# One visit of the multiplier for the last 64 middle units of two neighbouring expert blocks

## The chip, the cores and the metric

The kernel runs on one core of a Trainium2 chip. The core has a matrix engine (TensorE, "PE" in the profile; its weight loads are listed apart as "PEld"), a vector engine (VectorE, "DVE"), a scalar engine (ScalarE, "ACT"), a general engine (GpSimd, "POOL") and an engine that here only issues transfers (SyncE, "SP"). Each engine works through its own list in order; where one needs another's result it waits on a semaphore. Matrix results land in PSUM, eight banks that hold 128 x 512 float32 numbers each; everything else is in SBUF. The metric is device time in microseconds (us) of one execution.

## The reference: attention, then a mixture of nine experts

Shapes: `x` is 4 x 1024 x 256, that is 4096 tokens of width 256.

```python
x = x + xattn(ctx, layernorm(x), scale, shift)   # 16 heads, 77 keys a batch
h = layernorm(x)                                  # 4096 x 256
probs = softmax(h @ Wr)                           # 9 experts
w, idx = top_k(probs, 2); w = w / sum(w)
hidden = silu(h @ Wg[e]) * (h @ Wu[e])            # 704 middle units of expert e
out = x + sum over the token's two e of w_e * (hidden @ Wd[e])
```

All of it is float32. The 704 middle units are 5 x 128 + 64, and that odd 64 is what the change is about.

## The kernel before

The first part, up to some 340 us of the trace, is attention and routing: it finishes the new `x`, decides each token's two experts, and writes lists of tokens by expert into HBM. The second part works through 40 *blocks*. A block is a set of tokens with its experts; `blocks` (L1240 to L1257) holds the order as triples (token tiles, number, kind):

- *pair* blocks have 256 tokens of one expert, two token tiles `h` = 0, 1 of 128. There are 26: six early ones (blocks 0 to 5), whose places are known before all tokens are routed, and later ones of the kinds quad/quad2 (two neighbours that share one load of weights) and pair;
- *thin* blocks ("one") have 128 tokens of one expert;
- flex and quart blocks have 128 tokens of two or four experts, worked by column tiles of the multiplier.

The order of the kinds after the early blocks is the string at L1243, in which Q stands for quad, quad2; P for a pair, O for a thin block, F for flex, X for quart. Five more blocks (Q O Q O P) follow it.

Step `j` of the main loop does this. `fetch` (L1574) issues the loads: weights of block j+2, rows of tokens of block j+3, lists further ahead; SP issues weights in order, through `load` (L1338), into three buffers for Wg and Wu and four for Wd. `hidden_pair` (L1414) multiplies the block's turned tokens `xT` by Wg and Wu in six chunks `f`. A chunk is 128 middle units and fills a bank `pg`: ACT takes silu of one half (L1427), DVE multiplies it by the other half into `hid` (L1428). The sixth chunk has 64 units: 64 columns of Wg stand beside 64 of Wu, so one product gives gate on rows 0 to 63 and up on rows 64 to 127, and L1432 and L1433 make rows 64 to 127 of `hid[:, NF, :]` from it. Rows 0 to 63 of that slice are zeros, set once, and so are those of Wd's buffers.

Between chunks, DVE has other work in the same queue: in the early blocks `pump` (L1551) lets up to 12 instructions of the routing of the last token group and of the late blocks' tables go by after each chunk; from step 6 on, `turning` (L1389) gives it three 32 x 32-square transposes after each chunk, 16 a block, which turn the next block's tokens. In steps 1 to 5, `turn` (L1401) turns the next block's tokens on the multiplier instead, with four instructions into a PSUM bank `px`, after the block's `hidden_pair`.

Then, still in step j, `down(j - 1)` (L1508) multiplies the *previous* block's hidden units by Wd: for each token tile six accumulating products of 128 rows, `f` = 0 to 5, the last with the 64 rows of zeros. ACT scales the result by the token's weight (`co`, L1519) and POOL adds the rows into the output (`adding`, L1537). So PE always has twelve products of the block before to do while ACT and DVE finish the present block's last chunk. The schedule is written out by hand: the engines' queues are in the order of the calls.

PSUM: five banks in a ring (`mm_tile`, L133) for all `pg`, `px` and the routing's products, and three named banks: `sc0` for `px`, `sc1` and `sc2` for `down`.

Of the kernel before, what the change touches and what calls it, by code (L numbers as in the profile page):

```python
# [21 lines left out]
def kernel(  # L22
# [99 lines left out]

    ps_mm = ctx.enter_context(tc.tile_pool(name="ps_mm", bufs=5, space=bass.MemoryType.PSUM))
    ps_sc = ctx.enter_context(tc.tile_pool(name="ps_sc", bufs=1, space=bass.MemoryType.PSUM))
# [6 lines left out]
    BH = B // 2  # L131

    def mm_tile(name):  # L133
        return ps_mm.tile([P, TB], F32, tag="mm", name=name)

# [1106 lines left out]
    uppers, turn_set = {}, 0  # L1242
    order = "QO PF PO QX PO QF PF PO QX PO QF PF"  # L1243
    for step in order.replace(" ", ""):
# [11 lines left out]
    uppers[LAST] = [turn_set % SETS]  # L1256


    begun = {}
# [6 lines left out]
    wgus, downs, xTs, cos = {}, {}, {}, {}  # L1266
    hids, wds, yins, ids = [], [], [], []
    late = {}
# [14 lines left out]
    def open_experts():  # L1283
        for name, bufs in (("wpool", LEAD + 1), ("fpool", 1), ("spool", 2)):
            pools[name] = ctx.enter_context(tc.tile_pool(name=name, bufs=bufs))
        f = pools["fpool"]
        hids.extend(f.tile([P, NF + 1, TS], F32, name=f"hid{i}") for i in range(2))
        wds.extend(f.tile([P, NF + 1, D], F32, name=f"wd{i}") for i in range(NB_W))
        yins.extend(f.tile([P, 2, D], F32, name=f"yin{i}") for i in range(NB_Y))

        ids.extend(f.tile([P, b[0], WORDS], I32, name=f"ids{j}") for j, b in enumerate(blocks))
        for t in hids + wds:
            nc.gpsimd.memset(t[0:64, NF, :], 0.0)
        for t in yins:
            nc.gpsimd.memset(t, 0.0)
# [6 lines left out]
    def weights(j, in_parts=False):  # L1302
# [16 lines left out]
        at = PARTS[kind] * i  # L1319
        parts = load(tabs[kind][0][0:1, at : at + 1], w, d)  # L1320
        if in_parts:
# [15 lines left out]

    def load(number, w, d):  # L1338
        e = nc.values_load(number, engines=[mybir.EngineType.SP], min_val=0, max_val=E - 1)
# [13 lines left out]
        )  # L1353
        nc.sync.dma_start(
            out=d[64:128, NF, :], in_=wd[bass.ds(e, 1), NF * P : FF, :].rearrange("o p d -> (o p) d")
        )
        yield True
# [43 lines left out]
    def turn(j):  # L1401

        nh, xT = blocks[j][0], turned_tile(j)
        px = ps_sc.tile([P, TB], F32, tag="sc0", name=f"px{j}").rearrange("p (c t) -> p c t", c=C)
        for c in range(C):
# [8 lines left out]
    def hidden_pair(j, also={}, upcoming=iter(())):  # L1414

        (w,), xT, hid = wgus.pop(j), xTs.pop(j), hids[j % 2]
        for f in range(NF + 1):
# [13 lines left out]
            else:  # L1431
                nc.scalar.activation(sl[64:128, :], pg[0:64, 0, :], AF.Silu)  # L1432
                nc.vector.tensor_tensor(  # L1433
                    hid[64:128, NF, :], pg[64:128, 0, :], sl[64:128, :], ALU.mult
                )
            pump()
# [71 lines left out]
    def down(j):  # L1508
        ds, hid, nh = downs.pop(j), of(hids, j), blocks[j][0]
        co = cos[j] = pools["spool"].tile([P, 2, D], F32, tag="co", name=f"co{j}", bufs=3)  # L1510
        for h in range(nh):
            po = down_tile(j, h)
            for f in range(NF + 1):
                for d, rows in zip(ds, lanes(ds)):
                    at = slice(h * P + rows.start, h * P + rows.stop)
                    nc.tensor.matmul(  # L1516
                        po[rows, :D], hid[:, f, at], d[:, f, :], start=(f == 0), stop=(f == NF)
                    )
            nc.scalar.activation(  # L1519
                co[:, h, :], po[:, :D], AF.Copy, scale=ids[j].bitcast(F32)[:, h, 1:2]  # L1520
            )

    def down_tile(j, h):
# [213 lines left out]


    delayed = []
    for j in range(LAST):  # L1740
# [60 lines left out]
```

## Time and profile before

| | |
|---|---|
| time, median of 3 | 853.81 us (852.67 to 854.43) |
| the profiled execution | 852.54 us, span 850.8 us, granted TensorE clock 0.998 |
| PE busy | 840.8 us, 99% of the span |
| weight loads (beside PE) | 674.9 us, 79% |
| DVE busy | 596.7 us, 70% |
| ACT busy | 380.7 us, 45% |
| POOL busy | 313.1 us, 37% |
| DMA | 208 GB/s on average |

A group line gives line, engine, operation, names of output and input, the array's rows x columns, the operand's partitions x elements and the count, then total busy time and mean ns. A timeline line gives start, length, engine, line, operation, names, shapes, count, and in brackets the engine's idle time before it and what ended that. A float32 product of the program is two MATMUL records in the trace. Records of PE overlap, since its work is pipelined and its ends are modelled: the pace is read from one start to the next.

### The profile page before, as it was taken

The page shows a single profiled execution, that of the slowest core. Times are in us where ns is not written, and L with a number is a line of the kernel's source. Part 1 is how long each engine was busy: PE and PEld are TensorE (multiplying, and loading weights), DVE is VectorE, ACT ScalarE, POOL GpSimd, SP SyncE. Part 2 cuts the span into 40 slices and gives each one's busy share as a digit, 9 for nine tenths or more (in the row PEclk, how much of TensorE's full clock was granted, in tenths as well). Part 3 has the DMA queues.
Part 4 walks back from the last instruction along what each step waited for, and adds up shares of the span by engine and source line. Part 5 has one row for each costly group of instructions (what it writes and reads, how often), then busy time and mean ns, then how long its engine had stood idle before and what let it go on. Part 6 is the DMA issues. An engine that isn't in the chain of part 4 may idle for free. (4 is left out here: it accounts for less than half of the span.)

```text
span 850.8 us, 14468 instructions
## 1 busy us (share of the span) xinstructions
PE 840.8 (99%) x4148; PEld 674.9 (79%) x4148; DVE 596.7 (70%) x1887; ACT 380.7 (45%) x1570; POOL 313.1 (37%) x344
## 2 busy tenths in 40 slices
PE   9999999999999999999999999999999999999996
PEld 6755877877877878988888879788778878877895
DVE  5777779999989989454864675485578466667550
ACT  4878687978879686352222222222222222222221
POOL 3100000404424140477663444544434453453522
PEclk9999999999999999999999999999999999999999
DMA  8026656576565597996885799789779988788521
GB/s 294 3 106 182 173 180 203 160 222 197 159 203 175 158 274 222 299 303 138 224 246 132 192 343 358 185 244 330 189 228 347 283 228 281 214 246 254 114 26 19
DMA packets 129424, 177.25 MB, mean 208 GB/s; under 512 B 26167, under 2 KB 95295, under 8 KB 129216
## 3 DMA queue, kind: packets, MB, share of 16 engines
q1 hardware_dynamic: 111930, 158.57, 58.9%
q0 software_dynamic: 17344, 17.75, 11.9%
q8 instruction: 33, 0.54, 0.3%
q14 instruction: 47, 0.39, 0.1%
q10 hardware_dynamic: 70, 0.00, 0.0%
HBM read 136.89 MB, written 40.81 MB: 209 GB/s over the span
## 5 line engine op out<-in xcount | busy, mean ns | idle before, releaser
L1421 PE MATMUL pg<-xT,wgu 128*128 128x256 f32 x1100 | 242.7, 379 | 0.1
L1421 PEld LDWEIGHTS pg<-xT,wgu 128*128 128x128 f32 x1100 | 208.5, 190 | 28.8 <-ACT xT L1410 0.7
L1537 POOL DMA_INDIRECT out_dram<-co,ids x73 | 116.0, 1590 | 205.6 <-ACT co L1519 132.7
L300 ACT ACTIVATE ex<-psc,mx 128x77 f32<-128x77 f32 x512 | 159.4, 338 | 62.6 <-DVE mx L289 59.9
L1516 PE MATMUL po<-wd,hid 128*128 128x256 f32 (+2 forms) x768 | 173.2, 380 | 0.0
L1516 PEld LDWEIGHTS po<-wd,hid 128*128 128x128 f32 (+2 forms) x768 | 138.7, 183 | 28.6 <-issue 6.2
L1049 POOL DMA_INDIRECT list_d<-line,r_pli x64 | 68.9, 1077 | 230.4 <-DVE r_pli L1036 120.1
L361 PE MATMUL po<-u,aT 128*128 128x265 f32 x640 | 151.8, 392 | 0.0
L361 PEld LDWEIGHTS po<-u,aT 128*128 128x128 f32 x640 | 149.7, 311 | 2.6 <-ACT u L151 0.4
L1394 DVE STREAM_TRANSPOSE xT<-yin 32x128 f32<-32x128 f32 (+1 forms) x528 | 144.6, 274 | 9.0
L285 PE MATMUL psc<-g,zT 128*128 128x462 f32 (+1 forms) x384 | 146.7, 513 | 0.0
L1428 DVE TENSOR_TENSOR hid<-pg,sl 128x256 f32<-128x256 f32 x130 | 55.0, 424 | 117.0 <-ACT sl L1427 115.5
L1427 ACT ACTIVATE sl<-pg 128x256 f32<-128x256 f32 x130 | 49.8, 384 | 176.7 <-PE pg L1421 169.4
L300 ACT ACTIVATION_READ_ACCUMULATOR ex<-psc,mx 128x1 f32 x512 | 111.4, 218 | 0.0
L285 PEld LDWEIGHTS psc<-g,zT 128*128 128x128 f32 x384 | 69.7, 190 | 42.9 <-issue 34.3
L1519 ACT ACTIVATE co<-po,ids 128x256 f32<-128x256 f32 x66 | 31.2, 475 | 123.5 <-PE po L1516 123.5
L341 DVE STREAM_TRANSPOSE anT<-an 128x1280 f32<-128x1280 f32 x32 | 79.7, 2490 | 0.5 <-DMA a_d<-anT 0.4
L1361 POOL DMA_INDIRECT yin<-y_d,ids x66 | 69.3, 1051 | 28.2 <-issue 18.7
L289 DVE TENSOR_REDUCE mx<-psc 128x6 f32<-128x462 f32 (+1 forms) x96 | 53.6, 558 | 18.5 <-PE psc L285 18.5
L1506 DVE STREAM_TRANSPOSE hid<-hs 32x160 f32<-32x160 f32 (+1 forms) x112 | 39.5, 353 | 1.7
L322 DVE TENSOR_TENSOR an<-ex,rs 128x1024 f32<-128x1024 f32 x32 | 39.3, 1228 | 1.1
L1449 PEld LDWEIGHTS pt<-xT,wgu 128*128 128x128 f32 x308 | 35.1, 192 | 2.1 <-issue 2.0
(370 smaller groups left out, 767.9 us busy)
## 6 DMA issues: line engine op xcount, KB each, us to landing
wgu<-in_L_ffn_Wg_dram SPq DMA_DIRECT2D x33, 704.0 KB
wd<-in_L_ffn_Wd_dram SPq DMA_DIRECT2D x33, 640.0 KB
a_d<-anT SPq DMA_DIRECT2D x32, 640.0 KB
aT<-a_d SPq DMA_DIRECT2D x128, 160.0 KB
wgu<-in_L_ffn_Wu_dram SPq DMA_DIRECT2D x33, 512.0 KB
w_up<-in_L_ffn_Wg_dram SPq DMA_DIRECT2D x12, 704.0 KB
d_up<-in_L_ffn_Wd_dram SPq DMA_DIRECT2D x12, 640.0 KB
w_up<-in_L_ffn_Wu_dram SPq DMA_DIRECT2D x12, 512.0 KB
```

The lines of the kernel that those rows point to most:

```text
L285: nc.tensor.matmul(psc[:, :w], zT[:, c, :], g_sb[i // NS // GPB][:, c, h * J : h * J + w], start=(c == 0), stop=(c == C - 1),)
L289: nc.vector.tensor_reduce(nmx[i][:, h : h + n], psc[:, : n * J].rearrange("p (h j) -> p h j", h=n), AX.X, ALU.max, negate=True,)
L300: nc.scalar.activation(exs[i][:, h + q, :], pscs[k][:, q * J : (q + 1) * J], AF.Exp, bias=nmx[i][:, h + q : h + q + 1], accum_out=sms[i][: ...
L341: nc.vector.transpose(turned.rearrange("p q t k -> p q k t"), an_of[0].rearrange("p (k q t) -> p q k t", q=NQ, t=Q))
L361: nc.tensor.matmul(po[:, :DE], aT[:, :, n], u_sb[b][:, n, :], start=(n == 0), stop=(n == KC - 1))
L1049: i = nc.gpsimd.indirect_dma_start(out=list_d[:, :], out_offset=bass.IndirectOffsetOnAxis(ap=place_i[:, s : s + 1], axis=0), in_=entry.bit ...
L1361: return nc.gpsimd.indirect_dma_start(out=dst, out_offset=None, in_=src, in_offset=bass.IndirectOffsetOnAxis(ap=offsets, axis=0), **kw,)
L1394: yield nc.vector.transpose(xT[q : q + Q].rearrange("p c (h t) -> p h c t", t=P)[:, :nh, :, a : a + Q], of(yins, j)[a : a + Q].rearrange(" ...
L1421: nc.tensor.matmul(pg[:, g, :], w[:, c, at : at + P], xT[:, c, :], start=(c == 0), stop=(c == C - 1),)
L1428: made = nc.vector.tensor_tensor(hid[:, f, :], pg[:, 1, :], sl, ALU.mult)
L1516: nc.tensor.matmul(po[rows, :D], hid[:, f, at], d[:, f, :], start=(f == 0), stop=(f == NF))
L1537: i = nc.gpsimd.indirect_dma_start(out=out_r, out_offset=bass.IndirectOffsetOnAxis(ap=ids[j][:, h, word : word + 1], axis=0), in_=cos[j][: ...
```

## The change

Neighbouring pair blocks are joined two by two (`second_of`), taken greedily in the order of the blocks. In a joined block the last 64 middle units of token tile 0 are written to rows 0 to 63 of a new 128 x 128 buffer `end`, those of token tile 1 to rows 64 to 127: two DVE instructions of 64 x 128 in place of one of 64 x 256. The last 64 rows of Wd are loaded twice, to rows 0 to 63 and to rows 64 to 127. In `down(j)` of a join's first block four products of 64 rows now open the accumulation of both blocks' four token tiles; two use the upper half of the multiplier's rows, two the lower half, by turns. The ten products of 128 rows of each block follow, the first block's at once and the second block's in its own `down` a step later. The second block's two open banks are `sc0` and one bank taken from the ring, which therefore has four banks in the expert part and also serves `px`. The order of the kinds is written anew, so that two more couples of pair blocks are neighbours. There are ten joins: blocks 0+1, 2+3, 4+5; five quad couples; two couples of pairs.

```diff
+    mm_next = [0, 5]
+
     def mm_tile(name):
-        return ps_mm.tile([P, TB], F32, tag="mm", name=name)
+        mm_next[0] = (mm_next[0] + 1) % mm_next[1]
+        return ps_mm.tile([P, TB], F32, tag=f"mm{mm_next[0]}", name=name)
...
-    order = "QO PF PO QX PO QF PF PO QX PO QF PF"
+    order = "QO FPPO QX PPO QF PFPO QX PO QF F"
...
+    second_of = {}
+    for j in range(LAST - 1):
+        if blocks[j][0] == blocks[j + 1][0] == 2 and j not in second_of.values():
+            second_of[j] = j + 1
+    joined = {*second_of, *second_of.values()}
...
-        nc.sync.dma_start(
-            out=d[64:128, NF, :], in_=wd[bass.ds(e, 1), NF * P : FF, :].rearrange("o p d -> (o p) d")
-        )
+        for k in range(2 - copies, 2):
+            nc.sync.dma_start(
+                out=d[64 * k : 64 * k + 64, NF, :],
+                in_=wd[bass.ds(e, 1), NF * P : FF, :].rearrange("o p d -> (o p) d"),
+            )
...
-        px = ps_sc.tile([P, TB], F32, tag="sc0", name=f"px{j}").rearrange("p (c t) -> p c t", c=C)
+        px = mm_tile(f"px{j}").rearrange("p (c t) -> p c t", c=C)
...
-                nc.vector.tensor_tensor(
-                    hid[64:128, NF, :], pg[64:128, 0, :], sl[64:128, :], ALU.mult
-                )
+                to = [hid[64:128, NF, :]]
+                if j in joined:
+                    to = [of(ends, j)[64 * h : 64 * h + 64] for h in range(2)]
+                n = TS // len(to)
+                for h, t in enumerate(to):
+                    at = slice(h * n, (h + 1) * n)
+                    nc.vector.tensor_tensor(t, pg[64:128, 0, at], sl[64:128, at], ALU.mult)
...
     def down(j):
+        if j in second_of:
+            both = j, second_of[j]
+            for i in both:
+                for h in range(2):
+                    half = slice(64 * h, 64 * h + 64)
+                    ended[i, h] = down_tile(i, h) if i == j else held_tile(i, h)
+                    nc.tensor.matmul(
+                        ended[i, h][:, :D], of(ends, i)[half], (ds if i == j else downs[i])[0][half, NF, :],
+                        start=True, stop=False,
+                    )
         for h in range(nh):
-            po = down_tile(j, h)
-            for f in range(NF + 1):
+            po = ended.pop((j, h), None)
+            begun = po is not None
+            if not begun:
+                po = down_tile(j, h)
+            chunks = NF if begun else NF + 1
+            for f in range(chunks):
...
+    def held_tile(j, h):
+        if h:
+            return ps_mm.tile([P, TB], F32, tag="mm4", name=f"po{j}_{h}")
+        return ps_sc.tile([P, TB], F32, tag="sc0", name=f"po{j}_{h}")
...
+    mm_next[1] = 4
     delayed = []
     for j in range(LAST):
```

In `load`, `copies` is 2 for a joined block and 1 for any other.

## The prediction

> **What bounds the kernel now.** I read the page's busy times first, then the timeline of PE over the expert part, then DVE's timeline at the same places, then the groups by shape. The page:
>
> ```profile
> PE 840.8 (99%) x4148; PEld 674.9 (79%) x4148; DVE 596.7 (70%) x1887; ACT 380.7 (45%) x1570; POOL 313.1 (37%) x344
> ```
>
> PE is busy 99% of the span and its list of waits holds almost nothing: whatever the change takes off PE's list is gained, and whatever PE has to wait for is lost. PE's timeline at the ends of blocks 1, 3, 5 (the second blocks of the early joins) and around block 7 (second of the first quad couple):
>
> ```profile
> 368.87 0.60 PE L1407 MATMUL px<-ident,yin 128*128 128x128 f32 x4
> 369.31 5.35 PE L1516 MATMUL po<-wd,hid 128*128 128x256 f32 x24
> 374.75 5.45 PE L1421 MATMUL pg<-xT,wgu 128*128 128x256 f32 x24
> ...
> 400.57 5.35 PE L1516 MATMUL po<-wd,hid 128*128 128x256 f32 x24
> 405.75 9.66 PE L1421 MATMUL pg<-xT,wgu 128*128 128x256 f32 x44
> ...
> 430.80 5.34 PE L1516 MATMUL po<-wd,hid 128*128 128x256 f32 x24
> 435.98 4.26 PE L1421 MATMUL pg<-xT,wgu 128*128 128x256 f32 x19
> ```
>
> ```profile
> 450.66 9.66 PE L1421 MATMUL pg<-xT,wgu 128*128 128x256 f32 x44
> 460.16 5.34 PE L1516 MATMUL po<-wd,hid 128*128 128x256 f32 x24
> ```
>
> The pace is (460.16 - 450.66)/44 = 0.216 us a record, 0.432 a product. The 24 records after each block are the block *before*; they start with no wait. Now DVE's product for the last 64 units of those same blocks (L1433):
>
> ```profile
> 376.34 0.43 DVE L1433 TENSOR_TENSOR hid<-pg,sl 64x256 f32<-64x256 f32 x1
> ...
> 403.77 0.43 DVE L1433 TENSOR_TENSOR hid<-pg,sl 64x256 f32<-64x256 f32 x1
> ...
> 432.24 0.43 DVE L1433 TENSOR_TENSOR hid<-pg,sl 64x256 f32<-64x256 f32 x1
> ```
>
> ```profile
> 459.91 0.42 DVE L1428 TENSOR_TENSOR hid<-pg,sl 128x256 f32<-128x256 f32 x1 [0.54 <-ACT sl L1427]
> 460.37 0.74 DVE L1394 STREAM_TRANSPOSE xT<-yin 32x64 f32<-32x64 f32 x3
> 461.13 0.43 DVE L1433 TENSOR_TENSOR hid<-pg,sl 64x256 f32<-64x256 f32 x1
> ```
>
> It starts 7.0, 3.2 and 1.4 us after PE begins the `down` products of blocks 0, 2 and 4, and 0.97 us after it in block 7, behind three transposes; the four other second quad blocks show 0.94 to 0.95, and a pair block ahead of a thin one has the same three transposes. Today nothing of PE needs it for another block. Last, whether two half-height tiles run together, and what a change of tiling costs:
>
> ```profile
> L567 PE MATMUL pk<-cT,wk_sb 128*128 128x308 f32 x32 | 9.3, 429 | 0.3 <-ACT cT L514 0.3
> ...
> L719 PE MATMUL pgk<-kTs,wqT 64*128 64x308 f32 x64 | 9.0, 427 | 0.0
> ```
>
> ```profile
> 616.83 9.66 PE L1421 MATMUL pg<-xT,wgu 128*128 128x256 f32 x44
> 626.42 0.43 PE L1516 MATMUL po<-wd,hid 128*64 128x256 f32 x1
> ...
> 651.19 0.38 PE L1516 MATMUL po<-d_up,hid 128*64 128x256 f32 x1
> 651.50 5.18 PE L1449 MATMUL pt<-xT,wgu 128*128 128x128 f32 x44
> 656.51 5.35 PE L1516 MATMUL po<-wd,hid 128*128 128x256 f32 x24
> ```
>
> 64-row products take 9.0/64 = 0.141 each where 128-row ones of that width take 9.3/32 = 0.291: two do run in the time of one. Entering column tiles costs 0.09 (9.59 in place of 9.50) and 0.04 in the first record; leaving costs 0.10 before the next record (651.50 for 651.19 + 0.216) and 0.10 in the 44 that follow (5.01 where undisturbed ones take 4.91). I take these 0.13 and 0.20 for row tiles.
>
> **Part by part.** *Removed*: per join, four products with half their rows zero, 4 x 0.432 = 1.73 us of PE. *Added*: four 64-row products in two slots, 0.86. On PE's list alone ten joins would save 8.6, less 3.3 for twenty changes of tiling.
>
> *The new wait.* The four products stand first in `down` of the join's first block, directly behind the second block's `hidden_pair`. Products three and four read the second block's `end`, which DVE has not yet made. PE's list is in order, so behind them stand the first block's twenty records and the whole next `hidden_pair`; ACT's `co` and POOL's additions wait for those in turn. The cover that L1433 had, twelve products of another block, is gone.
>
> *Late joins (seven).* Time counted from the end of `hidden_pair`. DVE begins its last product at 0.97. A half of 64x128 I put at 0.29, between the 0.20 of routing's 128x36 and 0.43 of 64x256, and the second 0.26 after the first (back-to-back ones overlap: a row of two 128x256 takes 0.75, not 0.85): ready at 1.26 and 1.52. From a result to PE's first record is 0.23: ACT's copy at 374.11 lasts 0.59, the weight load begins at 374.74 (0.04), and the stretch from there to 384.79 is 0.18 longer than 44 x 0.216 plus 0.36 for routing's products. Then 0.43 for the fourth product: 2.18; leaving the tiling, 2.38. That replaces 1.73, so each join *loses* 0.65; seven lose 4.6. Lower end: no cost of leaving, 0.45 each, 3.2; upper end: each half as long as the whole and a switch twice as dear, about 1.1 each, 7.7. I take 4.6, as each term has a near row.
>
> *Early joins (three).* The same, from the three rows of L1433. Join 0+1: 376.34 + 0.55 + 0.23 + 0.43 + 0.20 = 377.75, plus 20 records (4.32) = 382.07, where 374.75 stood: +7.3. Join 2+3: 403.77 likewise gives 409.50 for 405.75: +3.75. Join 4+5: 432.24, plus 0.13 for block 4's product cut in two in a queue that is full, gives 438.10 for 435.98: +2.1. The second blocks' own `down` is shorter by 0.86; that counts after joins 0+1 and 4+5, while after 2+3 it only brings PE sooner to a wait that DVE ends. Sum 13.2 - 1.7 = 11.5. These DVE times don't move with the wait: before 376.34 stand ACT's three table loads and its 2.06 us of `y`, then routing steps from 370.26 on; before 403.77 and 432.24 up to 12 table steps per chunk. None needs a PE record later than its block's `hidden_pair`. Half a microsecond either way each: 10 to 13.
>
> *Costed at nothing.* The ring of four: `px` of block 2 now takes the bank of block 1's chunk 2, freed by a DVE product at 370.26, 1.8 us after PE asks; block 6's `px` waits likewise for a product at 430.86. Both waits lie inside the longer wait behind them; alone they would cost 1.8 each. In late blocks a bank is refilled four chunks (6.9 us) after it was filled and DVE frees it within 2. The fifteen further 64 KB loads: 1 MB, issued with their block's weights two steps ahead; uncovered, 3.8 us at 250 GB/s. SP's load of block 4's Wd waits for `down` of block 0 to free a buffer and moves with it; block 4 is a step and a half away. The new order: the same 45 loads; PE's one wait for a transfer in the whole expert part is 0.3 us.
>
> **Sum.** 11.5 + 4.6 = 16.1 on 852.54 of the profiled execution, 868.6. The median shown is 1.27 above that execution: 869.9.
>
> **Two rules against the rows.** The Trainium skill, TensorEngine Tiling (Array Packing), Key Properties, says that changing the tiling mode drains the engine; it gives no price. TensorE: Matmul & The Clock Gate, Part 2, puts the drain at about 128 cycles of 2.4 GHz; by that estimate ten exits cost 0.5 and not 2.0, and the sum would be 1.5 lower.
> The same page's Part 1 says that an idle window of some 3.4 us halves PE's clock until it has been busy as long; that speaks against this change, and by it the sum would be 1.7 to 3.4 higher.
>
> **Rivals.**
> 1. *A slow PE after the longest wait.* In join 0+1 PE would stand still from about 371.7 to 377.1. No wait of that length is in this trace. Its first twelve multiplications, after a standstill, took 5.49 us (L170), 0.46 each, over twice the pace. If PE slows for as much again, 12 records cost 12 x 0.24 = 2.9: 872.8.
> 2. *Row halves don't overlap in this use.* Products one and two hide in the wait; the fourth would follow the third, ready at 1.26 + 0.23 + 0.86 = 2.35 for 2.18: 0.17 a join, 871.6. Against it: L719.
> 3. *A late transfer.* P after P and F after F ask for their weights closer together; one load of 2.1 MB at 318 GB/s (640 to 680 us) is 6.6 us, so a load late by half that gives 873, a whole one 876. Against it: the 0.3 us.
> 4. *Other side: `end` is there when PE asks.* Then the list's saving stands, 8.6 - 3.3 = 5.3, and the time is 848.6. Place: DVE's queue before L1433. The waits of product three, counted from the end of products one and two, would have to total under 5.3; by the rows above they come to about 18 (7.0, 3.2, 1.5 and seven of 0.93). It needs DVE's other work to stand elsewhere in its queue, and the diff moves none of it.
>
> **How the numbers follow.** Forecast 0.60, its own range 866.5 to 873 from the bounds above; slow PE 0.20; no overlap 0.08; late transfer 0.07; in time 0.05. Range: from 864 (the lower ends and a little more) to 875 (rival 1, part of rival 3); outside lie rival 4, whole late loads and sums of upper ends, under 0.2. Slower by over 0.2% (about what a measurement can tell): 0.94; within: 0.01; faster: 0.05.
>
> **What would show it.** Weight loads of the tails (`end`) idle some 5, 3 and 1 us in the early joins and about 0.9 in each late one, ended by DVE; PE busy share down by about 2 points; 80 fewer full-height records of L1516 in its successor; DVE's halves near 0.29. Wrong if those waits are absent, or if PE's pace after the first is not 0.216.

## The result, and the profile after

The changed kernel takes 886.15 us (median of six, 885.36 to 886.73) where the kernel before, on the same chip, takes 853.33 (six, 852.67 to 854.43): a ratio of 1.0382, 95% interval 1.0371 to 1.0392. That is 32.8 us more. The prediction had the sign and 16.1 us, half of it, and the time lies outside its range. The profiled execution has a span of 884.9 us against 850.8, so 34.1 us are to be placed.

The page of the changed kernel, busy time of the engines and the granted TensorE clock in 40 slices:

```profile
PE 850.2 (96%) x4148; PEld 674.0 (76%) x4148; DVE 599.6 (68%) x1907; ACT 380.2 (43%) x1570; POOL 311.4 (35%) x344
PEclk9999999999999999988999999999999999998998
```

PE has *more* busy time than before (840.8), though its list should have saved some of it. Besides the last slice, in which the program ends, two stretches of the clock lie below 9, one at the early joins and one near the end. Its list of waits, which held almost nothing, now reads (engine, what waited, what ended it; us in total, times, longest):

```profile
PE po L1532 <- DVE end L1450: 11.2, 9, 4.6
PE pg L1432 <- DVE xT L1405: 5.1, 2, 3.9
PE pg L1432 <- ACT co L1549: 2.1, 2, 1.2
PE px L1418 <- issue: 1.8, 1, 1.8
PE px L1418 <- DVE hid L1439: 1.5, 1, 1.5
```

The first row is the wait that was predicted, and so are the last two, which the prediction took to be hidden. The second and third are not in the prediction at all. PE's timeline at the joins 0+1, 2+3 and 4+5 (L1532 are the products of 64 rows, L1545 the others of `down`):

```profile
373.96 0.63 PE L1418 MATMUL px<-ident,yin 128*128 128x128 f32 x4 [1.80 <-issue]
374.51 0.70 PE L1532 MATMUL po<-wd,end 64*128 64x256 f32 x4
379.83 1.54 PE L1532 MATMUL po<-wd,end 64*128 64x256 f32 x4 [4.62 <-DVE end L1450]
381.31 5.96 PE L1545 MATMUL po<-wd,hid 128*128 128x256 f32 x20
...
412.05 0.70 PE L1532 MATMUL po<-wd,end 64*128 64x256 f32 x4
415.69 1.54 PE L1532 MATMUL po<-wd,end 64*128 64x256 f32 x4 [2.94 <-DVE end L1450]
417.17 6.79 PE L1545 MATMUL po<-wd,hid 128*128 128x256 f32 x20
...
449.79 1.69 PE L1532 MATMUL po<-wd,end 64*128 64x256 f32 x8
```

Twenty records of L1545 take 4.48 at the usual pace; behind the two waits they take 5.96 and 6.79. Join 4+5 does not wait for `end` at all: its eight records go in one, because PE has already stood 1.49 us at `px`, just ahead of them, for a bank of the ring that DVE had still to read (the last row of the list). So nine of the ten joins wait for `end`. A late join is shorter and clean:

```profile
479.23 0.70 PE L1532 MATMUL po<-wd,end 64*128 64x256 f32 x4
480.46 1.02 PE L1532 MATMUL po<-wd,end 64*128 64x256 f32 x4 [0.53 <-DVE end L1450]
481.42 4.58 PE L1545 MATMUL po<-wd,hid 128*128 128x256 f32 x20
485.84 5.07 PE L1464 MATMUL pt<-xT,wgu 128*128 128x128 f32 x44
```

Stretches of the changed kernel: from and to, length, busy time of PE, PEld, DVE, ACT and POOL with their counts, then the granted PE clock, the DMA share and GB/s:

```profile
379.80:382.00 2.20, 2.17 (x6) 1.43 (x7) 0.29 (x1) 0.00 (x0) 0.00 (x0) 0.50 0.44 167
384.00:386.00 2.00, 2.00 (x10) 1.76 (x9) 0.00 (x0) 0.47 (x1) 0.10 (x1) 0.97 0.00 0
415.60:418.00 2.40, 2.31 (x6) 1.57 (x7) 2.06 (x12) 0.00 (x0) 1.79 (x3) 0.50 0.90 297
420.00:422.00 2.00, 2.00 (x7) 1.62 (x6) 0.00 (x0) 0.16 (x1) 0.00 (x0) 0.58 0.38 125
449.80:451.40 1.60, 1.60 (x9) 0.87 (x8) 0.87 (x3) 0.81 (x2) 0.00 (x0) 1.00 1.11 326
814.00:817.00 3.00, 3.00 (x9) 2.37 (x8) 2.89 (x9) 0.38 (x1) 0.48 (x1) 0.50 1.10 350
```

The clock is at half for some 4 to 6 us behind the waits of 4.62 and 2.94 and behind one near the end; behind the wait of 1.49 ahead of join 4+5 (449.80) it is full. The third slow place has nothing to do with a join. DVE's timeline there, and PE's record that follows:

```profile
798.94 5.87 DVE L1521 STREAM_TRANSPOSE hid<-hs 32x160 f32<-32x160 f32 x16
804.84 2.51 DVE L1405 STREAM_TRANSPOSE xT<-yin 32x128 f32<-32x128 f32 x8
...
808.82 2.52 DVE L1405 STREAM_TRANSPOSE xT<-yin 32x128 f32<-32x128 f32 x8
811.37 5.85 DVE L1521 STREAM_TRANSPOSE hid<-hs 32x160 f32<-32x160 f32 x16
```

```profile
811.60 12.71 PE L1432 MATMUL pg<-xT,wgu 128*128 128x256 f32 x44 [3.92 <-DVE xT L1405]
```

This is the block behind two neighbouring F blocks of the new order. Each F block hands DVE 16 transposes that turn its hidden units (L1521, 5.87 us; the *hidden turn*) besides the transposes of wide next blocks (2.5 us for eight). The hidden turn of the first F block (798.94) stands ahead of the transposes of `xT` in the queue. DVE has no gap left; the next block's `xT` is finished at 811.34, and PE stands from 807.68 on. Its 44 records take 12.71 where 9.66 is the rule.

So the 34.1 us are: ten joins 20.4 (among them 1.9 and 2.8 of half clock); the new order 10.3 (waits of 3.92, 1.21, 1.18 and 0.93 ahead of four blocks, 7.2, the first two ended by `xT` and the others by ACT's `co`; and 3.05 of half clock at 811.6); and 3.1 that are lost before block 0 begins (342.88 for 339.76). Sum 33.8.

### The profile page after: what moved, and what is told of

Same layout as the page of the kernel before. It is cut to its first block, busy times and chain, and to the rows that moved or that the text cites. A ratio compares the mean times of both kernels' runs of the same rounds, so it can differ in the third digit from the quotient of the medians.

```text
span 884.9 us, 14540 instructions
## 1 busy us (share of the span) xinstructions
PE 850.2 (96%) x4148; PEld 674.0 (76%) x4148; DVE 599.6 (68%) x1907; ACT 380.2 (43%) x1570; POOL 311.4 (35%) x344
## 4 chain that ended last, share of the span: by engine, by line
PE 70%; DVE 11%; issue 8%; DMA 5%; ACT 4%; POOL 2%; SPq 0%; POOLq 0%; DVEq 0%; ACTq 0%
PE pg L1432 20%; PE po L1545 13%; PE po L364 13%; PE psc L288 11%; DMA out_dram<-co,ids 4%; PE pt L1464 3%; ACT ex L303 2%; DVE anT L344 1%; PE po L1532 1%; POOL out_dram L1575 1%; PE psg L1501 1%; PE pgk L722 1%; PE pk L570 1%; PE psu L1501 1%; PE pv L796 1%
## 5 line engine op out<-in xcount | busy, mean ns | idle before, releaser
L1432 PE MATMUL pg<-xT,wgu 128*128 128x256 f32 x1100 | 245.9, 383 | 7.2 <-DVE xT L1405 5.1
L1432 PEld LDWEIGHTS pg<-xT,wgu 128*128 128x128 f32 x1100 | 210.8, 192 | 37.5 <-ACT co L1549 4.6
L1545 PE MATMUL po<-wd,hid 128*128 128x256 f32 (+2 forms) x688 | 160.4, 388 | 0.0
L1545 PEld LDWEIGHTS po<-wd,hid 128*128 128x128 f32 (+2 forms) x688 | 125.9, 187 | 30.2 <-issue 9.1
L1052 POOL DMA_INDIRECT list_d<-line,r_pli x64 | 66.7, 1042 | 233.2 <-DVE r_pli L1039 121.5
L1549 ACT ACTIVATE co<-po,ids 128x256 f32<-128x256 f32 x66 | 31.2, 473 | 141.0 <-PE po L1545 140.3
L1521 DVE STREAM_TRANSPOSE hid<-hs 32x160 f32<-32x160 f32 (+1 forms) x112 | 39.5, 353 | 1.7
```

The lines of the kernel that those rows point to most:

```text
L1052: i = nc.gpsimd.indirect_dma_start(out=list_d[:, :], out_offset=bass.IndirectOffsetOnAxis(ap=place_i[:, s : s + 1], axis=0), in_=entry.bit ...
L1432: nc.tensor.matmul(pg[:, g, :], w[:, c, at : at + P], xT[:, c, :], start=(c == 0), stop=(c == C - 1),)
L1545: nc.tensor.matmul(po[rows, :D], hid[:, f, at], d[:, f, :], start=(f == 0 and not begun), stop=(f == chunks - 1),)
```

## Experiments

The chips differ. On those of the following runs the kernel before takes 870 to 872 us, so each variant is set against the kernel before on its own chip; figures in expectations that were written from the first chip are read as differences. A second trace of the kernel before shows what the chip does.

**The kernel before, again** (no edit).

> The kernel before, unaltered, for a trace of it on a chip where it takes some 870 us, to set the other traces of such chips beside it. Theory (the 17 us against the first chip are lost at the first expert blocks, whose weights come late): TensorE stands still 10 to 17 us between 355 and 440 us, and is as on the first chip after that. Rival (a slower chip throughout): the span grows evenly over all stages.

Measured: 870.85 us, span 868.3. PE's timeline of the first expert blocks there:

```profile
376.77 1.50 PE L1421 MATMUL pg<-xT,wgu 128*128 128x256 f32 x2 [1.33 <-issue]
...
389.27 7.86 PE L1421 MATMUL pg<-xT,wgu 128*128 128x256 f32 x24 [4.21 <-ACT xT L1410]
```

PE stands still in pieces for 5.9 us within block 1 and once for 4.21, with slow records behind. The first theory is right on the place: the difference is in the early blocks. That weights come late there isn't shown: the pieces end in "issue", that is, the profile names no releaser for them. Cut every trace at three places (first `hidden_pair` record of block 0; first record `pt` of the first thin block, which is step 8; first chunk of the last block) and the stretch between the last two is the same on both chips to 0.1 us: 359.93 and 360.02. It is a ruler for everything that happens late. The early stretch is 125.6 on the first chip and 142.2 here and moves by some us from run to run, so little is read from it alone. The rest behind the third cut is 25.5 to 25.7 in all kernels.

| kernel | block 0 begins | early stretch | late stretch | ratio of times |
|---|---|---|---|---|
| before, first chip | 339.76 | 125.58 | 359.93 | |
| changed, first chip | 342.88 | 142.96 | 373.51 | 1.0382 |
| before, again | 340.60 | 142.17 | 360.02 | |
| changed, again | 342.60 | 161.82 | 373.60 | 1.0389 |
| order alone | 340.44 | 144.16 | 366.21 | 1.0104 |
| order alone, short hidden turn | 340.29 | 140.25 | 362.53 | 1.0021 |
| strict turn of five banks alone | 342.70 | 148.28 | 360.20 | 1.0006 |
| ring of four with px alone | 342.51 | 144.39 | 360.10 | 1.0060 |
| joins, old order | 341.60 | 160.68 | 362.43 | 1.0233 |
| late joins, new order | 342.62 | 150.20 | 374.01 | 1.0249 |
| half-height products last | 342.47 | 153.58 | 364.75 | 1.0173 |
| the same, old order | 341.74 | 150.83 | 356.53 | 1.0109 |
| late joins last, old order and banks | 342.08 | 143.67 | 356.52 | 0.9967 |

**The order alone.**

```
# before.py
-    order = "QO PF PO QX PO QF PF PO QX PO QF PF"
+    order = "QO FPPO QX PPO QF PFPO QX PO QF F"
```

> The kernel before with nothing but the new order of the kinds. Theory (the order itself fills DVE's queue: a wide block behind a block of several experts gets its turned tokens late): PE waits for xT ahead of blocks 10 and 11, ahead of 17 and, longest, some 4 us, ahead of block 35, with a stretch at half the granted clock after that last wait; together 7 to 11 us, 860 to 864. Rival (as the prediction had it, the order costs nothing, and those waits come from the joins): 853.3 within 1.

Measured: 881.07 us, ratio 1.0104, 95% interval 1.0071 to 1.0138, or +9.4 us. With no join at all the new order costs, and 6.2 us of it lie in the late stretch. PE's waits there are 5.6 us: 2.90 behind the two F blocks, 1.18, 1.05 and 0.47 at the places where the changed kernel has its own. What the prediction put at nothing is dear. Behind the 2.90 the clock stays at 1.00, so the half clock of the changed kernel is missing here.

**The order with a short hidden turn.** Is it DVE's queue, or the loads?

```
# before.py with the new order
-            for q in range(0, P, Q):
+            for q in (P - Q,):
```

> The kernel before with the new block order alone (1.010 of the kernel before), and of the sixteen VectorE transposes by which a block of four experts turns its hidden units (5.85 us) only four done (1.5 us), the other twelve left out, so that the values of these blocks are wrong. Theory (the new order costs because two wide blocks come one after the other, or a wide one next to pair blocks, and VectorE's queue then holds a hidden turn of 5.85 us ahead of the next block's xT, for which TensorE waits, 7 us in all and 3 us of half clock behind the longest): the waits for xT vanish, and it takes 0.998 to 1.003 of the kernel before. Rival (the order costs by its loads): still 1.007 or more.

Measured: 872.46 us, ratio 1.0021 (1.0004 to 1.0039). The record behind the F blocks, first with the order alone, then with the short turn:

```profile
805.87 9.73 PE L1421 MATMUL pg<-xT,wgu 128*128 128x256 f32 x44 [2.90 <-issue]
```

```profile
798.29 9.73 PE L1421 MATMUL pg<-xT,wgu 128*128 128x256 f32 x44 [1.26 <-issue]
```

The trace names no releaser, but in the first kernel DVE's last transpose of `xT` ends at 805.77. Of the 6.2 us in the late stretch 3.7 go with twelve of sixteen hidden transposes; every load is as it was. The waits shrink rather than vanish (2.3 us are left, 1.26 here and 1.06 ahead of block 10), since eight wide transposes of 2.5 us still stand in the queue; the two waits that ended with `co`, 1.18 and 0.47, are gone. In the late stretch loads are ruled out as the main cause.

**The joins without the order**, and **the late joins without the early ones**.

```
# after.py, joins in the old order
-    order = "QO FPPO QX PPO QF PFPO QX PO QF F"
+    order = "QO PF PO QX PO QF PF PO QX PO QF PF"
```

> The changed kernel with the order of before, so eight joins in place of ten. Theory: the waits for xT and the stretch of half clock ahead of block 35 are gone (7.2 and 3.0), and two late joins at 0.65 each: 886.2 - 11.5, about 874 to 876. Rival (the order is free): 886.2 - 1.3 = 884.9.

```
# after.py, late joins alone
-    for j in range(LAST - 1):
+    for j in range(EARLY, LAST - 1):
```

> The changed kernel, but the six early blocks are not joined; seven late joins stay. Theory: the 9.2, 5.7 and 1.8 us that the three early joins added are gone, less 0.9 of saving; the two waits of px for a bank of the ring of four, which those waits covered, show now (1.8 and 1.5); the doubled loads of blocks 0 and 1 no longer hold SP up while attention still runs (1.6): 886.2 - 15.9 + 3.3 - 1.6 = 872. Rival (as predicted, the early joins cost 11.5 with PE at its full pace): 874.7, less 1.6 if the loads count.

Measured: 892.38 us (1.0233, 1.0200 to 1.0267) and 893.76 us (1.0249, 1.0214 to 1.0284). Against the changed kernel's 1.0389 on a like chip (next runs) that is some 14 and 12 us less, where 11.5 and 14 were expected; for the second the intervals are too wide to choose between theory and rival. The late stretch in the old order is 362.43, 2.4 more than before. It holds four whole joins and of join 6+7 only the second block's shorter `down`, which saves 0.86: so the four cost 3.3, two of them 0.65 each, as in the changed kernel, the others 0.9 and 1.2, with short waits behind them. The late stretch of the second is that of the changed kernel (374.01 and 373.6), as it should be: with six joins at 0.65, the 0.86 of join 6+7, the order's 6.2, and, behind the two F blocks, 1.0 more of waiting (3.91 for 2.90) and 3 us of half clock that the order alone doesn't have, it adds up to 373.2 (360.0 + 3.9 - 0.9 + 6.2 + 1.0 + 3.0). In the early stretch the two show costs mixed with that chip's own stalls; I read no number for the early joins from them.

**The changed kernel again, and with the waits filled.** Here PE does idle-filling products in the place of waiting.

> The changed kernel once more, unaltered, beside the three variants run with it on one chip, because the chips differ: on the chip of the four runs before, the kernel before took 871.7 us where it took 853.3 us elsewhere. Theory (the change costs some 33 us by its new waits of TensorE and the half clock after them): 3.5 to 4 per cent slower where the kernel before takes 853 us; fewer, 2.3 to 3 per cent, on a chip where the early blocks stand still for late transfers in the kernel before too. Rival (a disturbance of that one chip): within 2 per cent of the kernel before.

```
# after.py, within the join's loop over the tiles
                     ended[i, h] = down_tile(i, h) if i == j else held_tile(i, h)
+                    for _ in range({0: 11, 2: 7}.get(j, 0) if i != j and h == 0 else 0):
+                        nc.tensor.matmul(
+                            ended[i, h][:, :D], hid[:, 0, :P], ds[0][:, 0, :], start=True, stop=True
+                        )
```

> The changed kernel with 11 idle-filling products of 128 rows by 256 columns ahead of product three of the first join (blocks 0 and 1), and 7 ahead of that of the second (2 and 3), written to the bank that the joined product then starts afresh; what is computed stays the same. They fill the 4.6 and 2.9 us in which TensorE waits for VectorE. Theory one (the half clock after those waits comes from TensorE standing idle): the granted clock after them stays near 1.0, the waits are replaced by busy time, and the time falls by 3 to 5 us against the changed kernel (the slow pace there was worth 1.9 and 2.8 us). Theory two (the low clock there has another cause, for instance the products of 64 rows): the clock still falls to 0.5 and the time stays within 1 us, or rises if the fillers delay the product.

Measured: 904.45 us (903.92 to 905.25; 1.0389 of the kernel before) and 900.49 us (900.10 to 902.25), 4.0 us less, although PE does 18 products more. Join 2+3 in the unaltered kernel and in the filled one (L1533 are the fillers, L1549 the `down` products):

```profile
433.51 1.55 PE L1532 MATMUL po<-wd,end 64*128 64x256 f32 x4 [4.31 <-DVE end L1450]
434.98 7.05 PE L1545 MATMUL po<-wd,hid 128*128 128x256 f32 x20
```

```profile
427.93 3.29 PE L1533 MATMUL po<-wd,hid 128*128 128x256 f32 x14
432.58 1.02 PE L1536 MATMUL po<-wd,end 64*128 64x256 f32 x4 [1.36 <-DVE end L1450]
433.53 4.58 PE L1549 MATMUL po<-wd,hid 128*128 128x256 f32 x20
```

```profile
432.60:436.00 3.40, 3.40 (x15) 2.77 (x16) 2.20 (x13) 0.00 (x0) 2.23 (x3) 1.00 0.94 299
```

The same products, behind the same operand, run at full clock when PE was kept at work. Twenty records take 4.58, not 7.05, and the products of 64 rows 1.02, not 1.55. The half clock is the price of standing still, and not of half-height products. This one join shows it, and makes 3.0 of the 4.0 us; at join 0+1 of this chip the clock is already low ahead of the fillers (0.60 from 385.6 to 386.6 us), behind a wait of 4.79 at `px`.

How long a stand it takes is not one number. A record of the kernel with the strict turn alone and one of the last kernel below (row tiles within blocks added):

```profile
444.72 11.45 PE L1424 MATMUL pg<-xT,wgu 128*128 128x256 f32 x44 [2.68 <-ACT xT L1413]
```

```profile
390.15 5.45 PE L1431 MATMUL pg<-xT,wgu 128*128 128x256 f32 x24 [3.42 <-ACT xT L1420]
```

Behind 2.68 us the clock is at 0.50 (446 to 448 us) and 44 records take 11.45 for 9.66; behind 3.42 it is 1.00 and 24 take the usual 5.45. In the clock records of all 17 traces the changes of the granted clock lie a multiple of 3.413 us apart, on a grid that has another phase in each trace, so that half clock lasts 3.41 us or a multiple of it. From 30 us on, a full clock fell at the end of every grid period in which PE, by its records, stood for 0.6 or more of the period, and of none with less than 0.53. The 2.68 us lie within one period; a border of the grid cuts the 3.42 in two halves, 0.48 and 0.52 of their periods.

**What stands ahead of the halves in DVE's queue.**

```
# after.py, hidden_pair
-            advance(upcoming, 3)
+            if not (f == NF - 1 and j in second_of.values() and j >= EARLY):
+                advance(upcoming, 3)
```

> The changed kernel without the three VectorE transposes that are queued between the second block's fourth chunk and its two halves, in the late joins; they are done after the halves. Theory (VectorE works in its queue's order, and what is queued ahead sets when the halves are made): the wait in a late join falls from 0.5 us to 0.2 or less, 1.5 to 3 us less in all over seven joins. Rival (ScalarE's activation or the product before it sets when the halves are made): within 0.5 us of the changed kernel.

Measured: 901.17 us (899.25 to 902.18), 3.3 less than the changed kernel beside it; the late stretch is 371.47, 2.1 less. A late join's wait:

```profile
495.18 1.02 PE L1533 MATMUL po<-wd,end 64*128 64x256 f32 x4 [0.16 <-DVE end L1450]
```

It falls from 0.51 to 0.54 us to 0.16 in each. Three transposes in DVE's queue are most of what PE waits for there.

**The half-height products last.** They go behind the first block's twenty records, which are ready.

```
# after.py, down(j), in outline
-        the joined products of 64 rows, then the first block's chunks 0 to 4
+        the first block's chunks 0 to 4, then the joined products of 64 rows,
+        then both copies to co
```

> The changed kernel with the products of 64 rows put behind the first block's ten products of 128 rows instead of ahead of them; the same products, loads, banks and block order. Theory (TensorE loses the time by standing at product three of each join until VectorE has made the second block's last half): the wait at that product goes in the seven late joins (0.5 us and some more each with the switch), and in the three early ones shrinks to what exceeds 4.5 us of products (4.6 + 2.9 us and the half clock after them, 4.7 us, mostly go): 12 to 22 us less than the changed kernel. The order's share, some 10 us, and the 3 us before block 0 stay, so it still takes 1 to 2 per cent more than the kernel before. Rival (the joins cost by the row tiles' own switches and pace): within 3 us of the changed kernel.

Measured: 886.78 us (881.54 to 889.35), 17.7 less than the changed kernel on that chip. A late join:

```profile
490.58 4.48 PE L1538 MATMUL po<-wd,hid 128*128 128x256 f32 x20
494.99 1.13 PE L1554 MATMUL po<-wd,end 64*128 64x256 f32 x8
496.05 5.18 PE L1464 MATMUL pt<-xT,wgu 128*128 128x128 f32 x44
```

All four products in one go, with no wait: 1.06 from start to start, for 1.73 before. A place in the list is worth about half of the loss: 8.2 us in that chip's early stretch and 8.9 in the late one, in which no wait for `end` is left.

**The same in the old order.**

```
# half-height products last
-    order = "QO FPPO QX PPO QF PFPO QX PO QF F"
+    order = "QO PF PO QX PO QF PF PO QX PO QF PF"
```

> The changed kernel with its joined products last and the block order of before (eight joins). Against the variant with the joined products last and the new order, which was 1.017 of the kernel before. Theory (the new order costs by itself 9 to 10 us, whatever the joins do): 1.003 to 1.010 of the kernel before. Rival (the order's cost and the joins' cost overlap in the same stalls): 1.013 or more.

Measured: 879.73 us, 1.0109 (1.0076 to 1.0142), between the two expectations. The late stretch says more than the total: 356.53, which is 3.5 *less* than in the kernel before. What is left over lies ahead of it, with block 0 and the early blocks.

**The banks.** First the strict turn of five banks alone, then four of them with `px` in the ring, as the change has it.

```
# before.py
+    mm_next = [0, 5]
...
     def mm_tile(name):
-        return ps_mm.tile([P, TB], F32, tag="mm", name=name)
+        mm_next[0] = (mm_next[0] + 1) % mm_next[1]
+        return ps_mm.tile([P, TB], F32, tag=f"mm{mm_next[0]}", name=name)
```

> The kernel before, with its five ring banks under five names taken in strict turn as in the changed kernel; px stays in its own bank, and nothing else differs. Theory: the strict turn meets banks that ACT has not yet emptied in the attention part, so block 0 begins 1.4 us later: 854.7. Rival (the 1.4 us is scatter of executions): 853.3.

```
# the same, and
-        px = ps_sc.tile([P, TB], F32, tag="sc0", ...)
+        px = mm_tile(f"px{j}")
...
+    mm_next[1] = 4
```

> The kernel before, with none of the joins and with its own block order, and of the change only the banks: strict turn instead of a free choice among five, four of them in the expert blocks, and the turned rows px taken from the same ring. Theory (the ring costs by itself, in two places: a later start of block 0, and px waiting for a bank whose product ScalarE or VectorE still reads): block 0 starts 2 to 3 us later than in the kernel before, px of block 2 waits 2 to 5 us and that of block 6 about 1.5, and it takes 4 to 9 us more than the kernel before (1.005 to 1.010). Rival (the early blocks of such a chip stand still for their weights anyway, and the waits for banks are hidden in that, as with the strict turn alone, 1.0006): 0.998 to 1.003.

Measured: 872.79 us, 1.0006 (0.9990 to 1.0022); and 875.86 us, 1.0060 (1.0033 to 1.0088), some 5 us more. ACT's and PE's timelines of the second:

```profile
378.64 2.06 ACT L966 ACTIVATE y<-x,fo,r_r 128x256 f32<-128x256 f32 x4
380.71 1.28 ACT L1430 ACT_TABLE_LOAD   x1
382.01 0.66 ACT L1430 ACTIVATE sl<-pg 128x256 f32<-128x256 f32 x2
```

```profile
376.09 2.08 PE L1424 MATMUL pg<-xT,wgu 128*128 128x256 f32 x4 [5.16 <-DVE hid L1431]
382.95 1.09 PE L1410 MATMUL px<-ident,yin 128*128 128x128 f32 x4 [4.79 <-issue]
383.83 6.98 PE L1519 MATMUL po<-wd,hid 128*128 128x256 f32 x24
```

With no join, `px` of block 2 waits 4.79 us for a bank whose chunk ACT reads only at 382.01, behind `y` and a table load; the clock is at 0.50 from 374 us, ahead of this wait, until 387. The ring costs by itself, as the theory had it. The strict turn alone can't be told from no change on such a chip. But block 0 begins later in it: the kernels with strict turns start at 341.4 to 342.9 us; of the seven with the old banks six start at 339.8 to 340.6, and the last (late joins last) at 342.1, with a wait of 1.41 for a transfer of `aT`. What PE waits for ahead of block 0 in the changed kernel, on the first chip, and not in the kernel before:

```profile
PE po L364 <- DMA aT<-a_d: 1.4, 1, 1.4
PE pu L811 <- ACT u L154: 0.6, 2, 0.3
PE pct L501 <- ACT cn L494: 0.6, 1, 0.6
PE pur L811 <- ACT urem L154: 0.5, 1, 0.5
```

The waits at `pu` and `pur`, 1.1 us between 54 and 75 us, stand in all ten traces with a strict turn and in none of the seven without, so they are the turn's. The waits for `aT` (up to 1.4) and `cn` (0.6 to 1.0) come in some traces and not in others, with the turn and without it. Together they are the 3.1 us. Doubled loads of the first blocks are not it: the late joins alone have none and begin at 342.62.

**Two row tiles without a neighbour.** Each pair block joins the halves of its own two tiles, behind its own products.

```
# before.py, down(j) of a pair block from block 2 on, in outline
-        per tile: chunks 0 to 4 and the last 64 units
+        per tile: chunks 0 to 4; then tile 0's last 64 units on rows 0 to 63
+        and tile 1's on rows 64 to 127
```

> The kernel before, with its block order, its ring of five banks and no block joined to another: each pair block from block 2 on multiplies the last 64 middle units of its own two tiles in two row tiles, behind its own twenty products of 128 rows. Eight products of 64 rows by 256 columns are replaced by two pairs of row tiles per block: 0.86 us of products removed (two at 0.43), against one switch in and out (0.13 and 0.20 us) and the second load of 64 KB. Theory (the gain of the row tiles is real, and it was the wait for the other block, the order and the banks that lost): some 13 to 15 pair blocks at 0.2 to 0.5 us each, 2 to 7 us less than the kernel before. Rival one (the doubled loads of 64 KB delay the blocks' weights): 0 to 10 us more. Rival two (switch and drain eat the gain): within 1.5 us.

Measured: 868.13 us, ratio 0.9977 (0.9960 to 0.9994), some 2 us less. The late stretch is 358.55, 1.45 less over some 17 pair blocks: under 0.1 each, below the 0.2 to 0.5 expected. The total is at the lower end of the theory, the trace agrees with rival two: one switch in and out for one product saved nearly eats the gain.

**The joins kept, the three losses taken away.** The products of 64 rows last, the old order, the old banks, and no joins among the early blocks; `sc0`, unused by `px` in the late blocks, and one bank of the ring hold the second block's sums. A second kernel adds the row tiles within blocks that have no partner.

```
# half-height products last, and
-    order = "QO FPPO QX PPO QF PFPO QX PO QF F"
+    order = "QO PF PO QX PO QF PF PO QX PO QF PF"
...
-    for j in range(LAST - 1):
+    for j in range(EARLY, LAST - 1):
...
-        return ps_mm.tile([P, TB], F32, tag=f"mm{mm_next[0]}", name=name)
+        return ps_mm.tile([P, TB], F32, tag="mm", name=name)
...
-        px = mm_tile(f"px{j}")
+        px = ps_sc.tile([P, TB], F32, tag="sc0", ...)
```

> The kernel before with its own block order and its own ring of banks, and five joins (none among the early blocks), whose eight products of 64 rows stand behind the first block's products of 128 rows. The second block's open sums lie in sc0, which no px uses by then, and in one bank of the ring. Measured from the first light product of a thin block (pt) to the last block's first chunk, this late stretch took 360.0 us in every trace with the old order and no join (359.9 to 360.2 over four traces), 362.4 with the changed kernel's joins in the old order and 356.5 with the joined products last. Theory (order, early joins and banks were the losses, the row tiles a gain): late stretch 356 to 357.5, block 0 and the early blocks as in the kernel before, 3 to 4.5 us less than the kernel before (0.995 to 0.9965). Rival (the joins gain only where the ring of four is there too, and a bank taken from the ring stalls the next block's chunks): 359 or more, no gain.

> The same, and every other pair block from block 2 on multiplies its own two tiles' last 64 units in two row tiles. Theory (the kernel with these alone took 0.9977 of the kernel before; its late stretch was 358.55, 1.45 less): a little less again where blocks are not joined, 0.5 to 1.5 us under late_last. Rival (one switch per block eats that gain): within 0.5 us of it.

Measured: 868.74 us, ratio 0.9967 (0.9951 to 0.9983), and 867.66 us, ratio 0.9961 (0.9945 to 0.9976). The two ends of the late stretch in the kernel before (first chip) and in the first of these:

```profile
465.34 5.08 PE L1449 MATMUL pt<-xT,wgu 128*128 128x128 f32 x44
...
825.27 3.62 PE L1421 MATMUL pg<-xT,w_up 128*128 128x256 f32 x16
```

```profile
485.75 5.18 PE L1461 MATMUL pt<-xT,wgu 128*128 128x128 f32 x44
...
842.27 3.62 PE L1429 MATMUL pg<-xT,w_up 128*128 128x256 f32 x16
```

359.93 has become 356.52, as expected. The joins gain 3.4 us in the late stretch once they wait for nothing: 0.66 in each of the four whole joins in it, and 0.76 in what lies in it of join 6+7. Both kernels are faster than the kernel before by some 0.35%, and than the changed one. The additional row tiles bring 0.4 in the late stretch, as their rival had it; the totals don't tell the two apart.

## Why the prediction was right and wrong

*The new wait: right, in place and length, at nine joins of ten.* It stands at product three and DVE ends it; at join 4+5 the wait at `px`, which was to be hidden behind it, hides it instead. A late join loses 0.65 us net, as worked out: 0.09 more in the second block's `hidden_pair`, 1.42 more in the first block's `down`, 0.86 less in the second's. The halves take 0.293 us for 0.29 predicted; two row tiles run side by side (eight records of 64 rows in 1.06 us, in the variant with these products last), so the second rival falls. Early joins, predicted +7.3, +3.75 and +2.1, measured +9.2, +6.6 and +1.8, of which the excess of the first two is the half clock behind the wait: 1.48 and 2.31 in the twenty records, 0.5 each in the products of 64 rows.

*The clock: a rival, and too small.* The prediction gave rival 1 a chance of 0.20, for join 0+1 alone, at 2.9 us. It happens three times: 1.9, 2.8 and 3.05 us, 7.7 in all. The rule that stood beside it, of the Trainium skill, TensorE: Matmul & The Clock Gate, Part 1 (an idle window of some 3.4 us, half clock for as long), was the better guide in kind: the clock changes on a grid of 3.413 us here. The traces differ in that a period need not be idle throughout; 0.6 of it is enough. So how a wait lies on the grid counts as much as its length: 2.68, 2.76 and 2.94 us halved the clock, 2.90, 3.13 and 3.42 did not, and the place at 811.6 cost 1.8 in place of 3.05 in the changed kernel's second trace (44 records in 11.42). That three waits were hit, and for how long, is in part luck. Filling the early waits brought 4.0 back.

*The new order: the step that failed most.* It was costed at nothing because "the same 45 loads" are issued. What moved with the order is not loads but DVE's transposes: an F block owes DVE 5.9 us of hidden turn, and two such blocks in a row, or one such block (F or X) ahead of two pair blocks, leave no gap. 7.2 us of waits, 5.1 of them for `xT`, and 3.05 of half clock; with no other edit, 9.4 us with an interval of 6 to 12; and most of it in the late stretch goes with the hidden turn. Rival 3 looked for trouble with the order in the weights' transfers, where it wasn't.

*The ring of four: costed at nothing behind a cover.* That `px` of block 2 would wait 1.8 was exact (1.80) and it was covered on the first chip, by the longer wait at product three. But the cover was the change's own wait; on a chip where ACT comes later it is 4.79. The turn itself costs 1.1 us of waits in the attention, at `pu` and `pur`; that wasn't seen, as the attention wasn't looked at. Ahead of block 0 3.1 us are lost in all; the other 2.0 are waits for `aT` and `cn`, which other traces have with and without the turn. The doubled loads, also costed at nothing, showed no cost: the kernel in which every pair block from block 2 on joins its own two tiles doubles them for all of these blocks, and gains.

Sum of what was missed: 4.7 (clock at two joins) + 10.3 (order) + 3.1 (ahead of block 0) = 18.1, on 16.1 predicted: 34.2 of 34.1 us.

*"Each join loses"* was true of these joins, not of joins: last in the list, the same products gain.

## What to carry to other kernels

An operand that another engine makes in passing should be asked for last, behind everything that is ready: the same four products lost 0.65 us a late join in front and gained 0.66 behind. When blocks are put in another order, follow each engine's own queue through the new neighbours, above all the one that turns data between blocks, and not only the loads. A cost that is hidden by a wait is not hidden once that wait is mended.

## What the runs showed of the hardware

- The granted TensorE clock fell to 0.50 during waits of 2.94, 3.92 and 4.62 us of the changed kernel and stayed there for 4 to 6 us of work; it was 1.00 behind a wait of 1.49. There is no border in the wait's length: 2.68 us was enough in one trace, 3.42 not in another. The clock changes on a grid of 3.413 us, and fell from full at the end of each period of it in which PE stood for 0.6 or more, and of none with less than 0.53. Products that compute nothing of use keep the clock up (join 2+3 with fillers, 1.00).
- Eight weight loads and products of 64 rows by 256 columns in two row tiles take 1.06 us from start to start, 0.133 a record, for 0.216 of a full-height one; with the change of tiling this leaves 0.66 us of 1.73 saved for two blocks together, where a block that changes the tiling anyway follows, and 0.47 where none does (join 6+7); where only two products are paired it leaves under 0.1 per block.
- The same program takes 853 us on one chip and 870 on others. Of 17.5 us between two traces 16.6 lie in the first expert blocks and 0.8 ahead of them; the late stretch agrees to 0.1 us. Why the early blocks are slower on the others stays open.
